# Placing the sums of four groups together in a graph layer: sets, 384-node parts and program order

## The chip, the cores and the metric

One Trainium2 chip, one of its cores. The metric is the device time of one execution in microseconds, the median of several runs. TensorE is called PE, its weight loads PEld, VectorE DVE, ScalarE ACT, GpSimd POOL, SyncE SP.

## What is computed

```python
h = jnp.maximum(_layernorm(x, axis=-1), 0.0)            # x: (12500, 256)
agg = jax.ops.segment_sum(h[src], dst, num_segments=N)  # 200000 edges, dst sorted
z = (1.0 + eps_gin) * h + agg
t = jnp.dot(z, W1) + b1                                 # 256 -> 512
t = jax.nn.relu(_batchnorm(t, g1, bt1))                 # statistics over all nodes
conv_out = jnp.dot(t, W2) + b2                          # 512 -> 256
out = x + jax.nn.relu(_batchnorm(conv_out + h, g2, bt2))
```

All numbers are float32. The edges come sorted by their destination `dst`; `src` is random. A flag computed on the chip selects the function `fast()` where the sorted destinations lie close enough to their expected places, which they do here, and `general()` otherwise.

## The kernel before

The 200000 edges are cut into 1563 tiles of 128 edges and these into 131 groups of 12 tiles (`GT`). Since the destinations are sorted and evenly spread, group `i` touches nodes near `96 * i` (`STEP`); a window of 280 nodes (`WIDE`) with a margin of 76 on the low side holds them. The nodes are cut into 25 chunks of 512 (`CH`) for everything else.

The first part of `fast()` is one loop over the groups, in which all the stages run at once:

- `h_chunk(g)` makes `h` of a chunk: statistics on DVE, 4 activations on ACT (both in `settle`, L328 to L339), a store of `h` to the table `h_tab` in DRAM, 8 transposes on PE (L365), their copies to `hc` on ACT and DVE (L369, L371), and a store of `hc` to `h_cols` by SP's queue (L372).
- `gather(i)` issues 12 indirect DMAs on POOL (L382), one for each tile: 128 rows of 1 KB each into one `gt` buffer, of which there are five (`AHEAD + 1`). The first 24 groups (`LEAD`) read `x` and are normalized by `settle` after they land; the others read `h_tab`.
- `sums(i)` makes a one-hot matrix `oh` of the 12 tiles on DVE (L407) and adds up the rows of equal destination with 12 matmuls (L417) into a PSUM tile `ps`. A float32 matmul gives two records in the trace.
- `join(i)` copies the sums to `zs` on ACT (L424) and makes a second one-hot matrix `at` on DVE (L426) that tells where in the window each destination lies; `put(i)` multiplies the two on PE (L436) into `pz`, which holds the sums by node, in columns.
- `z_chunk(c)` loads a chunk of `h_cols` by SP's queue (L395) and scales it by 1 + eps on ACT (L396); `add(i, pz)` adds `pz` to the one or two chunks that the window meets, on DVE (L449).
- `first_layer(c)` multiplies a complete chunk by W1 (L458), takes statistics on DVE (L462), copies the result on ACT (L463) and stores it to `t_tab` (L464).

The statistics are then aggregated (`norm`, L230 to L241). The second part loads `t_tab` and `h_cols`, normalizes on ACT (L510), multiplies by W2 (L517), adds `h` (L521) and takes statistics (L522). The third part loads `x`, normalizes (L536), transposes back on PE (L542), adds `x` (L548) and stores the output.

The order of the work inside the first part is set by a scheduler that the framework runs when the kernel is built: it may move an instruction on its engine past others of a later call. Waits between engines are semaphores: a tile's reader waits for its writer, and who takes a buffer again waits for its last reader. The lines of the loop are

```python
if i + AHEAD < NG:
    gather(i + AHEAD)
pz = None
if i > 0:
    join(i - 1)
    pz = put(i - 1)
if i < NG:
    if i < LEAD:
        settle(gathered[i], GT // 2, GT, gathered[i], "g")
    sums(i)
```

Of the kernel before, what the change touches and what calls it, by code (L numbers as in the profile page):

```python
# [7 lines left out]
F32 = mybir.dt.float32  # L8
I32 = mybir.dt.int32
# [9 lines left out]
MARGIN = 76  # L19
AHEAD = 4  # L20
# [9 lines left out]
def kernel(  # L30
# [233 lines left out]
    def fast():  # L264

        parts = []
        for n0, w in chunks:
            n = w * R
            parts.append([(c, min(P, n - c * P)) for c in range(-(-n // P))])

        def pieces(g):

            whole = sum(rows == P for _, rows in parts[g])
            yield 0, whole, P
            for c, rows in parts[g][whole:]:
                yield c, c + 1, rows

        def carry(eng, sb, table, g, store):
            n0 = chunks[g][0]
            for c0, c1, rows in pieces(g):  # L280
                if c0 == c1:
                    continue
                side = table[n0 + c0 * P : n0 + (c1 - 1) * P + rows, :].rearrange("(c p) d -> p c d", p=rows)
                if store:
                    eng.dma_start(side, sb[:rows, c0:c1, :])
                else:
                    eng.dma_start(sb[:rows, c0:c1, :], side)

        with ExitStack() as fs:
            keep = fs.enter_context(tc.tile_pool(name="keep", bufs=1))  # L290

            h_cols = dram.tile([NCH, P, DC, CH], F32, name="h_cols")
            t_tab = dram.tile([NCH, P, HC, CH], F32, name="t_tab")
# [4 lines left out]
            with ExitStack() as es:  # L298
# [3 lines left out]
                zcp = es.enter_context(tc.tile_pool(name="zc", bufs=4))  # L302
                tsp = es.enter_context(tc.tile_pool(name="ts", bufs=2))
                ps_h = es.enter_context(tc.tile_pool(name="ps_h", bufs=1, space=PSUM))
                ps_i = es.enter_context(tc.tile_pool(name="ps_i", bufs=1, space=PSUM))
                ps_s = es.enter_context(tc.tile_pool(name="ps_s", bufs=2, space=PSUM))
                ps_z = es.enter_context(tc.tile_pool(name="ps_z", bufs=1, space=PSUM))
                ps_t = es.enter_context(tc.tile_pool(name="ps_t2", bufs=2, space=PSUM))

                col_i = keep.tile([P, WIDE], I32, name="col_i")  # L310
                nc.gpsimd.iota(col_i, pattern=[[1, WIDE]], base=0, channel_multiplier=0)
                col = ps_i.tile([P, WIDE], F32, name="col")
# [7 lines left out]
                nc.vector.tensor_scalar(shift, shift, row, None, op0=OP.add)  # L320
# [24 lines left out]
                def x_chunk(g):  # L345
                    if g >= NCH:
                        return
                    n = chunks[g][1] * R
                    xts[g] = ln.tile([P, R, D], F32, name="xt", bufs=4)
                    if n < CH:  # L350
                        nc.vector.memset(xts[g], 0.0)
                    carry(nc.sync, xts[g], x, g, store=False)

                def h_chunk(g):
                    n = chunks[g][1] * R
                    slots = len(parts[g])
# [3 lines left out]
                    carry(nc.scalar, ht, h_tab, g, store=True)  # L360
                    hc = ln.tile([P, DC, CH], F32, name="hc")
                    for d in range(DC):
                        ph = ps_h.tile([P, CH], F32, name="pc")
                        for c in range(slots):
                            nc.tensor.transpose(  # L365
                                ph[:, c * P : (c + 1) * P], ht[:, c, d * P : (d + 1) * P], ident
                            )
                        if d % 2:
                            nc.scalar.copy(hc[:, d, :n], ph[:, :n])  # L369
                        else:  # L370
                            nc.vector.tensor_copy(hc[:, d, :n], ph[:, :n])  # L371
# [429 lines left out]
```

## Time and profile before

| | |
|---|---|
| median of 3 runs | 2610.4 us (2606.39 to 2611.99) |
| the profiled execution's own time | 2577.98 us |
| its span, first to last instruction | 2576.2 us |
| busy: PE, PEld, DVE, ACT, POOL | 1418.7, 1010.7, 714.3, 460.5, 1482.6 us |
| mean granted PE clock | 0.754 of full speed |
| HBM read, written | 284.26 MB, 64.00 MB |

A row of the costliest groups reads: line, engine, operation, the tiles out<-in, their shape, xcount, then busy us and mean ns of one, then the engine's idle time just before these instructions and what ended most of it. "issue" is time in which the engine waited for nothing that the profile shows; "remote" is a wait whose end the profile can't place with an instruction. A row of the waits reads: who waited <- for whom: us in total, times, the longest. A row of the timeline reads: start, length, engine, line, operation, tiles, xcount, and in brackets the idle time before it and its end. The ends of matmuls are modelled.

### The profile page before, as it was taken

The page shows a single profiled execution, that of the slowest core. Times are in us where ns is not written, and L with a number is a line of the kernel's source. Part 1 is how long each engine was busy: PE and PEld are TensorE (multiplying, and loading weights), DVE is VectorE, ACT ScalarE, POOL GpSimd, SP SyncE. Part 2 cuts the span into 40 slices and gives each one's busy share as a digit, 9 for nine tenths or more (in the row PEclk, how much of TensorE's full clock was granted, in tenths as well). Part 3 has the DMA queues.
Part 4 walks back from the last instruction along what each step waited for, and adds up shares of the span by engine and source line. Part 5 has one row for each costly group of instructions (what it writes and reads, how often), then busy time and mean ns, then how long its engine had stood idle before and what let it go on. Part 6 is the DMA issues. An engine that isn't in the chain of part 4 may idle for free.

```text
span 2576.2 us, 14802 instructions
## 1 busy us (share of the span) xinstructions
PE 1418.7 (55%) x4873; PEld 1010.7 (39%) x4873; DVE 714.3 (28%) x1060; ACT 460.5 (18%) x871; POOL 1482.6 (58%) x1575
## 2 busy tenths in 40 slices
PE   1265566545356455455545554464564555578985
PEld 1243444434244334344333443342443343353444
DVE  4355455222122112221211221221221122133444
ACT  1364566300000000000000000000000000014444
POOL 4666566666666666666666666666666666620000
PEclk6677787777678777777767777676787777788996
DMA  5566675333333333333334333333333333338539
GB/s 164 155 205 201 199 222 171 93 119 113 92 117 118 120 92 119 112 94 116 120 88 122 117 114 95 119 114 92 116 120 119 92 115 101 96 108 319 200 120 319
DMA packets 150067, 349.41 MB, mean 136 GB/s; under 512 B 28920, under 2 KB 84366, under 8 KB 143838
## 3 DMA queue, kind: packets, MB, share of 16 engines
q0 software_dynamic: 75008, 204.90, 27.4%
q1 hardware_dynamic: 44182, 91.21, 10.3%
q10 hardware_dynamic: 30792, 52.26, 5.4%
q8 instruction: 41, 0.67, 0.1%
q14 instruction: 44, 0.36, 0.0%
HBM read 284.26 MB, written 64.00 MB: 135 GB/s over the span
## 4 chain that ended last, share of the span: by engine, by line
another core or an unknown queue 49%; PE 29%; ACT 7%; issue 6%; DVE 4%; DMA 3%; SPq 0%; POOL 0%; ACTq 0%; DVEq 0%; POOLq 0%
PE ps L417 12%; PE py L517 7%; PE pz L436 5%; PE ph L458 4%; ACT gt L339 3%; DMA out_dram<-ot 1%; ACT zs L424 1%; ACT ht L339 1%; DVE oh L407 1%; DVE st L462 1%; DMA zc<-h_cols 1%; DVE zc L449 1%; PE pc L365 1%; ACT ts L463 1%
## 5 line engine op out<-in xcount | busy, mean ns | idle before, releaser
L382 POOL DMA_INDIRECT gt<-h_tab,srcT x1275 | 1207.5, 947 | 608.5 <-issue 370.9
L417 PE MATMUL ps<-gt,oh 128*128 128x256 f32 x3126 | 776.9, 409 | 55.5 <-ACT gt L339 42.8
L417 PEld LDWEIGHTS ps<-gt,oh 128*128 128x128 f32 x3126 | 654.2, 210 | 175.3 <-ACT gt L339 46.6
L436 PE MATMUL pz<-at,zs 128*128 128x280 f32 x524 | 207.2, 531 | 735.3 <-ACT zs L424 578.7
L407 DVE TENSOR_TENSOR oh<-col,dstT 128x1536 f32<-128x1536 f32 x131 | 229.0, 1748 | 1144.1 <-remote 857.0
L436 PEld LDWEIGHTS pz<-at,zs 128*128 128x128 f32 x524 | 119.4, 244 | 796.8 <-ACT zs L424 601.3
L382 POOL DMA_INDIRECT gt<-in_x_dram,srcT x288 | 273.5, 949 | 154.0 <-issue 79.9
L458 PE MATMUL ph<-zc,w1s 128*128 128x512 f32 (+1 forms) x400 | 218.2, 699 | 252.2 <-ACT ts L463 231.9
L424 ACT COPY zs<-ps 128x256 f32<-128x256 f32 x131 | 48.8, 373 | 1633.8 <-remote 1261.3
L458 PEld LDWEIGHTS ph<-zc,w1s 128*128 128x128 f32 x400 | 88.7, 230 | 362.4 <-ACT ts L463 247.0
L449 DVE TENSOR_TENSOR zc<-pz,zc 128x560 f32<-128x560 f32 (+9 forms) x203 | 100.8, 526 | 350.4 <-remote 267.6
L517 PE MATMUL py<-tT,w2s 128*128 128x512 f32 (+1 forms) x400 | 170.9, 590 | 12.0 <-ACT tT L510 12.0
L339 ACT ACTIVATE gt<-gt,nbg,rsg 128x256 f32<-128x256 f32 x288 | 149.5, 590 | 4.0 <-DVE nbg L337 1.9
L517 PEld LDWEIGHTS py<-tT,w2s 128*128 128x128 f32 x400 | 76.8, 193 | 106.0 <-issue 87.2
L462 DVE BATCH_NORM_STATS2 st<-ph 128x6 f32<-128x512 f32 (+1 forms) x100 | 66.6, 679 | 139.5 <-PE ph L458 74.8
L328 DVE BATCH_NORM_STATS2 stg<-gt 128x6 f32<-128x512 f32 x144 | 91.4, 689 | 34.2 <-DMA gt<-in_x_dram,srcT 31.2
L510 ACT ACTIVATE tT<-ti,of,sc 128x512 f32<-128x512 f32 (+1 forms) x100 | 72.0, 791 | 101.1 <-issue 86.7
L463 ACT COPY ts<-ph 128x512 f32<-128x512 f32 (+1 forms) x100 | 57.4, 575 | 181.4 <-DVE st L462 150.4
L426 DVE TENSOR_SCALAR at<-col,shift 128x280 f32<-128x280 f32 x131 | 65.4, 499 | 0.3 <-PE pz L436 0.3
L521 DVE TENSOR_TENSOR yT<-py,yT 128x512 f32<-128x512 f32 (+1 forms) x50 | 33.9, 679 | 110.5 <-PE py L517 108.5
L365 PE MATMUL pc<-ident,ht 128*128 128x128 f32 x196 | 39.2, 334 | 40.6 <-DVE hc L371 16.8
L542 PE MATMUL po<-ident,yr 128*128 128x128 f32 x196 | 40.3, 394 | 33.5 <-ACT yr L536 33.5
(74 smaller groups left out, 382.9 us busy)
## 6 DMA issues: line engine op xcount, KB each, us to landing
t_tab<-ts ACTq DMA_DIRECT2D x24, 1024.0 KB
ti<-t_tab SPq DMA_DIRECT2D x24, 1024.0 KB
gt<-h_tab,srcT POOLq DMA_INDIRECT x1275
xt<-in_x_dram SPq DMA_DIRECT2D x24, 512.0 KB
h_tab<-ht ACTq DMA_DIRECT2D x24, 512.0 KB
h_cols<-hc SPq DMA_DIRECT2D x24, 512.0 KB
zc<-h_cols SPq DMA_DIRECT2D x24, 512.0 KB
yT<-h_cols SPq DMA_DIRECT2D x24, 512.0 KB
```

Source lines behind the costliest of these rows:

```text
L328: nc.vector.bn_stats(st[:, c : c + 2, :].rearrange("p c s -> p (c s)"), v[:, c : c + 2, :].rearrange("p c d -> p d c"),)
L339: nc.scalar.activation(to[:, c, :], v[:, c, :], AF.Relu, bias=nb[:, c : c + 1], scale=rs[:, c : c + 1])
L382: nc.gpsimd.indirect_dma_start(out=ga[:rows, t - t0, :], out_offset=None, in_=x if i < LEAD else h_tab, in_offset=bass.IndirectOffsetOnAxi ...
L407: nc.vector.tensor_tensor(oh[:, :n, :], col[:, :P].unsqueeze(1).to_broadcast([P, n, P]), dstT[:, t0 : t0 + n].unsqueeze(2).to_broadcast([P ...
L417: nc.tensor.matmul(ps, lhsT=oh[:rows, j, :], rhs=ga[:rows, j, :], start=(j == 0), stop=(j == n - 1))
L424: nc.scalar.copy(zs, summed.pop(i))
L436: nc.tensor.matmul(pz[:, d, :WIDE], lhsT=zs[:, d * P : (d + 1) * P], rhs=at, start=True, stop=True)
L449: nc.vector.tensor_add(side, pz[:, :, a - lo : b - lo], side)
L458: nc.tensor.matmul(ph[:, :n], lhsT=w1s[:, d, f * P : (f + 1) * P], rhs=zc[c][:, d, :n], start=(d == 0), stop=(d == DC - 1),)
L462: nc.vector.bn_stats(st1[:, f, c, :], ph[:, :n])
L463: nc.scalar.copy(ts[:, f, :n], ph[:, :n])
L517: nc.tensor.matmul(py[:, :n], lhsT=w2s[:, f, d * P : (d + 1) * P], rhs=tT[:, f, :n], start=(f == 0), stop=(f == HC - 1),)
```

## The change

Four groups in a row form a set (`SET`), and the nodes are cut into 33 parts of 384 (`PART`), shifted by the margin of 76, so that set `s` belongs to part `s`. The six groups whose windows reach into a part (`REACH`) are placed with 12 matmuls into one PSUM tile, each over the blocks of 128 nodes that it can touch; one DVE instruction makes all 12 blocks of the second one-hot matrix (`spots`). `h` is no longer transposed in `h_chunk`: `h_rows` loads the rows of a part from `h_tab` by ACT's queue, `turn` transposes them on PE, `turn_out` copies them, scaled, to `zc` and, unscaled, to `hc` and stores that. `hold` copies the four groups' sums out of PSUM. The first layer works on a part in one PSUM tile of three banks; `take` reads it. `add` is called one set after `place`, and `take` one set after `first_layer`. The one-hot tile `oh` has four buffers instead of two. The scheduler is switched off for the first part (`manual_schedule`): each engine keeps program order. The second and third parts loop over the 33 parts instead of 25 chunks. The diff, cut to its core:

```diff
+SET = 4
...
+        PART = SET * STEP
+        NS = -(-NG // SET)
+        PB = PART // P
+        for j in [0] + [j for j in range(-SET, SET) if j]:
+            lo, hi = max(STEP * j, 0), min(STEP * j + WIDE, PART)
+            if lo < hi:
+                REACH.append((j, lo // P, -(-hi // P)))
...
-                zcp = es.enter_context(tc.tile_pool(name="zc", bufs=4))
-                tsp = es.enter_context(tc.tile_pool(name="ts", bufs=2))
-                ps_h = es.enter_context(tc.tile_pool(name="ps_h", bufs=1, space=PSUM))
+                zcp = es.enter_context(tc.tile_pool(name="zc", bufs=3))
+                tsp = es.enter_context(tc.tile_pool(name="ts", bufs=1))
+                ps_s = es.enter_context(tc.tile_pool(name="ps_s", bufs=SET // 2, space=PSUM))
...
-                ps_s = es.enter_context(tc.tile_pool(name="ps_s", bufs=2, space=PSUM))
                 ps_z = es.enter_context(tc.tile_pool(name="ps_z", bufs=1, space=PSUM))
-                ps_t = es.enter_context(tc.tile_pool(name="ps_t2", bufs=2, space=PSUM))
+                ps_t = es.enter_context(tc.tile_pool(name="ps_t2", bufs=1, space=PSUM))
+                es.enter_context(tc.manual_schedule())
...
-                    xts[g] = ln.tile([P, R, D], F32, name="xt", bufs=4)
+                    xts[g] = ln.tile([P, R, D], F32, name="xt", bufs=3)
...
-                    hc = ln.tile([P, DC, CH], F32, name="hc")
-                    for d in range(DC):
-                        ph = ps_h.tile([P, CH], F32, name="pc")
-                        for c in range(slots):
-                            nc.tensor.transpose(
...
-                    nc.sync.dma_start(h_cols[g, :, :, :n], hc[:, :, :n])
...
-                    oh = sel.tile([P, GT, P], F32, name="oh")
+                    oh = sel.tile([P, GT, P], F32, name="oh", bufs=SET)
...
-                    ps = ps_s.tile([P, D], F32, name="ps")
+                    if i % 2 == 0:
+                        summed[i // 2] = ps_s.tile([P, 2, D], F32, name="ps")
+                    ps = summed[i // 2][:, i % 2, :]
...
+                def h_rows(s):
+                    hrs[s] = ln.tile([P, PB, D], F32, name="hr")
+                    for c in ragged(s):
+                        nc.vector.memset(hrs[s][:, c, :], 0.0)
+                    part(nc.scalar, hrs[s], h_tab, s, store=False)
+                def turn(s):
+                    hr = hrs.pop(s)
+                    hc = ln.tile([P, DC, PART], F32, name="hc")
+                    zc[s] = zcp.tile([P, DC, PART], F32, name="zc")
+                    pz = ps_z.tile([P, DC, CH], F32, name="pz")
+                    for d in range(DC):
+                        for c in range(PB):
+                            nc.tensor.transpose(
+                                pz[:, d, c * P : (c + 1) * P], hr[:, c, d * P : (d + 1) * P], ident
+                            )
+                    turned[s] = hc, pz
+                def turn_out(s):
+                    hc, pz = turned.pop(s)
+                    nc.scalar.activation(zc[s], pz[:, :, :PART], AF.Copy, scale=gin1)
+                    nc.scalar.copy(hc, pz[:, :, :PART])
+                    nc.scalar.dma_start(h_cols[s], hc)
+                    h_rows(s + 2)
+                def hold(s):
+                    for i in range(s * SET, min((s + 1) * SET, NG)):
+                        held[i] = sel.tile([P, D], F32, name="zs", bufs=2 * SET)
+                        nc.scalar.copy(held[i], summed[i // 2][:, i % 2, :])
+                def spots(s):
+                    at = sel.tile([P, PAIRS, P], F32, name="at")
+                    nc.vector.tensor_tensor(
+                        at, col.unsqueeze(1).to_broadcast([P, PAIRS, P]),
+                        spot[:, s, :].unsqueeze(2).to_broadcast([P, PAIRS, P]), op=OP.is_equal,
                     )
...
+                def place(s):
+                    at = ats.pop(s)
+                    placed[s] = ps_z.tile([P, DC, CH], F32, name="pz")
...
                     for d in range(DC):
...
+                        for i, b0, b1, k in some:
+                            nc.tensor.matmul(
+                                placed[s][:, d, b0 * P : b1 * P], lhsT=held[i][:, d * P : (d + 1) * P],
+                                rhs=at[:, k : k + b1 - b0, :].rearrange("p b n -> p (b n)"),
+                                start=(i == some[0][0]), stop=(i == some[-1][0]),
+                            )
+                def add(s):
+                    nc.vector.tensor_add(zc[s], placed.pop(s)[:, :, :PART], zc[s])
+                def first_layer(s):
+                    layers[s] = ps_t.tile([P, HC * PART], F32, name="ph")
                     for f in range(HC):
...
+                        e = f * PART
+                        while e < (f + 1) * PART:
+                            end = min((e // CH + 1) * CH, (f + 1) * PART)
+                            for d in range(DC):
+                                nc.tensor.matmul(
+                                    layers[s][:, e:end], lhsT=w1s[:, d, f * P : (f + 1) * P],
+                                    rhs=zc[s][:, d, e - f * PART : end - f * PART],
+                                    start=(d == 0), stop=(d == DC - 1),
+                                )
+                            e = end
+                def take(s):
+                    ts = tsp.tile([P, HC, PART], F32, name="ts")
+                    a, b = there[s]
+                    ph = layers.pop(s)
+                    for f in range(HC):
+                        nc.vector.bn_stats(st1f[:, f, s, :], ph[:, f * PART + a : f * PART + b])
+                    nc.scalar.copy(ts.rearrange("p f n -> p (f n)"), ph)
+                    nc.scalar.dma_start(t_tab[s], ts)
...
+                for s in range(NS):
+                    for i in range(s * SET, min((s + 1) * SET, NG)):
+                        while made < NCH and made < 3 + NCH * i // (LEAD - AHEAD):
+                            h_chunk(made)
+                            made += 1
+                        if i == 0:
+                            h_rows(0)
+                            h_rows(1)
+                        if i + AHEAD < NG:
+                            gather(i + AHEAD)
                         if i < LEAD:
                             settle(gathered[i], GT // 2, GT, gathered[i], "g")
                         sums(i)
...
+                    spots(s)
+                    if s > 0:
+                        add(s - 1)
+                    if s > 1:
+                        take(s - 2)
+                    turn(s)
+                    hold(s)
+                    turn_out(s)
+                    if s > 0:
+                        first_layer(s - 1)
+                    place(s)
+                add(NS - 1)
+                take(NS - 2)
+                first_layer(NS - 1)
+                take(NS - 1)
...
-                name="ps_o", bufs=3, space=PSUM
+                name="ps_o", bufs=2, space=PSUM
```

## The prediction

> **What bounds the kernel now.** I first read the page's busy shares and its costliest groups. No engine is full, and the row at the top is GpSimd's gather:
>
> ```profile
> PE 1418.7 (55%) x4873; PEld 1010.7 (39%) x4873; DVE 714.3 (28%) x1060; ACT 460.5 (18%) x871; POOL 1482.6 (58%) x1575
> L382 POOL DMA_INDIRECT gt<-h_tab,srcT x1275 | 1207.5, 947 | 608.5 <-issue 370.9
> L417 PE MATMUL ps<-gt,oh 128*128 128x256 f32 x3126 | 776.9, 409 | 55.5 <-ACT gt L339 42.8
> L436 PE MATMUL pz<-at,zs 128*128 128x280 f32 x524 | 207.2, 531 | 735.3 <-ACT zs L424 578.7
> ```
>
> One gather takes 0.947 us and 0.30 us of issue, so 1.252 us start to start; a group of 12 takes 15.03 us, and all 1563 would take 1957 us. They actually run from 32.4 to 2275.4, 2243 us: some 286 us are stops. Second view, busy time by stretch, cut at the events that divide the stages (first gather, first gather from h_tab, last gather, first second-layer matmul, its end):
>
> ```profile
> 32.40:462.70 430.30, 224.46 (x803) 163.97 (x804) 209.21 (x392) 218.08 (x463) 273.49 (x289) 0.72 0.61 193
> 462.70:2275.40 1812.70, 938.47 (x3297) 698.69 (x3297) 371.10 (x473) 125.73 (x243) 1207.43 (x1275) 0.74 0.36 109
> 2275.40:2326.00 50.60, 37.44 (x149) 27.84 (x148) 17.11 (x33) 6.73 (x16) 0.06 (x1) 0.90 0.32 122
> 2326.00:2495.40 169.40, 169.40 (x393) 75.69 (x394) 66.51 (x96) 71.16 (x99) 0.00 (x0) 0.98 0.57 210
> 2495.40:2576.20 80.80, 41.74 (x205) 38.65 (x203) 34.18 (x39) 36.08 (x51) 0.00 (x0) 0.69 0.89 298
> ```
>
> The columns are length, then busy us of PE, weight load, DVE, ACT, POOL, then granted clock, DMA share, GB/s. The 24 groups gathered from x cost 17.9 us each, the 107 from h_tab 16.94 each (67.8 for four). So the second stretch loses 1.9 us a group, 205 us in all, against POOL's pace; that is what there is to win. Third, the waits say who stands there:
>
> ```profile
> ACT zs L424 <- remote: 1261.3, 68, 37.0
> DVE oh L407 <- remote: 857.0, 67, 22.7
> PE pz L436 <- ACT zs L424: 578.7, 57, 36.1
> POOL gt L382 <- remote: 198.2, 41, 6.4
> ```
>
> And the timeline shows one such place:
>
> ```profile
> 1189.83 5.34 PE L417 MATMUL ps<-gt,oh 128*128 128x256 f32 x24
> ...
> 1208.92 0.95 POOL L382 DMA_INDIRECT gt<-h_tab,srcT  x1 [0.30 <-issue]
> 1214.05 0.37 ACT L424 COPY zs<-ps 128x256 f32<-128x256 f32 x1 [25.46 <-remote]
> 1214.05 1.76 DVE L407 TENSOR_TENSOR oh<-col,dstT 128x1536 f32<-128x1536 f32 x1 [22.06 <-remote]
> 1214.29 0.94 POOL L382 DMA_INDIRECT gt<-h_tab,srcT  x1 [4.42 <-remote]
> 1214.48 2.23 PE L436 MATMUL pz<-at,zs 128*128 128x280 f32 x4 [19.30 <-ACT zs L424]
> ```
>
> PE's last sums stand as ended at 1195.2. ACT, DVE and POOL, which all wait for PE there, go on together at 1214.05: 19 us later, and 4.2 us after POOL's last gather ended. This repeats: releases come 2 to 6 us after POOL has stopped, or, in its longest runs of 45 us, once in the middle. So **PE's results are seen late while gathers stream**, by 8 to 22 us in about half of the groups. Each time PE stands with the next placement at its head, which needs ACT's copy of those sums. It runs about four groups behind the gathers, the five gt buffers are full, and POOL stops.
>
> [...] the sums' records start 0.43 us apart after the 19 us wait and 0.2155 later, and the clock averages 0.74. [...] POOL's 1.252 us is a pace that this change leaves alone.
>
> **The change, part by part**, for a set of four groups.
>
> *PE, at full clock.* Sums stay: 96 records at 0.2155 = 20.7. Placement was 16 records of 280 columns at about 0.236, 3.8 us. Now it is 24: eight each of 384, 256 and 128 columns. By columns 0.323 and 0.2155; [...]: 5.8 us. The first layer over 384 nodes was 5.2 (16 records at 0.43 per 512 nodes); in one PSUM tile across bank borders it is also 24 records, 5.8. The six transposes move here from h_chunk, 1.2. Sum 33.5 against 30.9, at clock 0.74 45.3 us, below POOL's 60.1: covered as long as PE isn't kept waiting.
>
> *ACT, DVE, SP and POOL.* From ACT go one hc copy a chunk (0.58) and the zc scaling of a loaded tile (1.15); it gains two copies of 768 columns (0.87 each, between its 0.585 and 1.145 rows) and one ts copy of 1536 instead of four (about 1.4). DVE makes one at of 1536 columns (1.76) for four of 280 (4 x 0.50), one add of 768 (about 0.95) for some six of 0.526, and no hc copy. Both were busy 371 and 126 of 1813 us in the second stretch: nothing there. SP loses the h_cols store and zc load, ACT's queue gains the h_tab load and h_cols store, at 0.33 to 0.46 us an issue, about 1 us a set. The bytes cancel (one 12.8 MB read for another). POOL is moved past nothing.
>
> *Waits.* oh has four buffers, so the one-hot waits for sums four groups back. add(s-1) and take(s-2) read PE results a set, some 60 us, old, longer than any lag seen. But hold(s) and turn_out(s) still read results that PE has just issued, and place(s) needs both. That is **one late wait a set instead of up to one a group**. Behind place in PE's order stand the next four sums, and POOL waits for their buffers. The lag W is bounded by 0 and 22 us; first_layer(s-1), 7.8 us at clock 0.74, now lies in front of place and covers that much. The copies before place are 4 x 0.373 + 2 x 0.87 = 3.2. So PE's set is 45.3 + 3.2 + W = 48.5 + W; with 8 to 22 less the cover, W is 0 to 14 and PE needs 49 to 63. POOL needs 60.1, plus 4.1 for a stop. Full rounds of stops give 64.2, none 60.1. I take half: 62.2. The 26.75 sets then take 1664 instead of 1813: **-149**.
>
> *The first stretch.* ACT and DVE keep program order through chunk, group and set. A chain of one group: 12 activations 7.1, the chunk's stretch with four of 0.59 beside six DVE statistics of 0.69, about 4.3, four hand-overs 1.6, a quarter chunk more, 0.8; a set's copies and its wait for sums and transposes, some 15, add 3.8. That is 17.6 against 17.9; bounds 16.5 to 20, so -34 to +50. I take +8, since each hold may also meet a lag.
>
> *The end.* After the last gather, 50.6 now: first_layer(31) and place(32) stand before the last add, take and first layer, and four aggregations read 198 instead of 150 numbers: about +6. Second layer: 528 records at 0.323 = 170.5 against 169.4. Output is at 89% DMA share with the same bytes: +1, between 0 and +8 since two po buffers replace three. Together +8.
>
> The profiled execution took 2578.0 us around its span of 2576.2, 32 below the median of 2610.4; I make the sum on the profile's terms and apply it to the median: 2610 - 149 + 8 + 8 = **2477, given as 2475**. Its own range is 2440 (lags vanish in most sets, 61) to 2540 (a stop in every set, 64.2, and a slower first stretch).
>
> **The rivals.** *POOL at its own pace*: 60.1 a set, -205 + 16: 2420; 2385 if the first stretch falls to 16.5. For it: before, releases came in mid-stream in every run of 45 us, and a buffer may wait some 45 us for its release here. Against: PE still has one fresh result to wait for, and no stretch of gathers over 45 us without a stop is seen.
>
> *PE becomes the bound, slower than before*: the sums' results lag 22 us in each set, and the first layer covers nothing because its own PSUM or add is late. Then PE needs 48.5 + 22 = 70.5 against 67.8 now: 26.75 x 2.7 = +72, with the +8 +8: 2698. It decides from W = 19.3 on. For it: hold, turn_out and place follow each other in one set, nothing else may be put into the gap under program order, and a clock at half makes the work itself 67. Against: the lag ended each time POOL stopped, and then everything older is released at once.
>
> *The set order doesn't matter*: lags are short but the five gt buffers still fill, one stop per two groups: 60.1 + 8.2 = 68.3, time 2610 + 13 + 16 = 2640.
>
> **Numbers.** Chances: the likeliest 0.48, POOL's pace 0.18, PE bound 0.24, no gain from the set 0.10. A measurement of this kernel can tell about 0.2%, 5 us, from no change. Faster 0.66; of the last case 0.03 falls within; slower 0.31. The range leaves a tenth on each side: 2385 to 2680.
>
> **What would show it.** Right: stops of POOL (idle before L382 beyond the 0.30 issue) fall from 286 us to about 130; stretches of 48 gathers with at most one stop; ACT's remote wait before zs drops to one per set; PE's wait stands in front of place. Wrong: the four-group period stays at 68 or more, with PE's idle time before place above 19 us a set; or the stretch from x takes over 480 us; or the end after the last gather takes over 320.

## The result, and the profile after

The changed kernel takes 2692.0 us (2688.8 to 2695.7) against 2608.4 (2606.4 to 2612.0): **3.2% slower**, ratio 1.0319, interval 1.0299 to 1.0340. The forecast was 2475.

One fact is needed to read the later numbers. The same two kernels were measured again, and whole series of runs came out in one of two conditions: in one the kernel before takes 2594 to 2614 us, as on record; in the other 2271 to 2272 us. I call them **held** and **free**; the traces below show why. Chips 1, 6 and 12 were seen free, 11 and 12 held, so the condition isn't the chip. The pair on record is held. Every number below stands beside the kernel before of its own series.

The profiled execution of after spans 2693.5 us. Its page, first the busy line, then the costliest groups (count, busy us and mean ns, then the engine's idle us just before them and what ended it):

```profile
PE 1565.6 (58%) x5653; PEld 1138.9 (42%) x5653; DVE 641.3 (24%) x853; ACT 476.4 (18%) x868; POOL 1480.9 (55%) x1577
L412 POOL DMA_INDIRECT gt<-h_tab,srcT x1275 | 1204.9, 945 | 726.3 <-issue 373.7
L436 PE MATMUL ps<-gt,oh 128*128 128x256 f32 x3126 | 753.1, 402 | 214.1 <-issue 157.2
L512 PE MATMUL ph<-zc,w1s 128*128 128x256 f32 (+2 forms) x792 | 304.3, 474 | 494.3 <-issue 488.2
L495 PE MATMUL pz<-at,zs 128*128 128x384 f32 (+2 forms) x780 | 268.4, 501 | 329.9 <-ACT hc L466 140.3
```

GpSimd's busy time is what it was, its idle time is 118 us longer. PE's wait in front of the placement fell from 735 to 330 us. The first layer stood like this before:

```profile
L458 PE MATMUL ph<-zc,w1s 128*128 128x512 f32 (+1 forms) x400 | 218.2, 699 | 252.2 <-ACT ts L463 231.9
```

Its 252 us have become 494, and nearly all of it is now put down to issue: no wait for a semaphore shows in front of these matmuls. Busy time by stretch, same cuts and columns as before:

```profile
32.00:447.70 415.70, 216.24 (x728) 163.26 (x728) 187.12 (x339) 212.22 (x439) 273.86 (x288) 0.77 0.53 169
447.70:2378.60 1930.90, 1084.71 (x4001) 802.98 (x4001) 318.62 (x286) 128.17 (x216) 1204.87 (x1275) 0.72 0.36 108
2378.60:2432.30 53.70, 40.10 (x169) 30.66 (x169) 11.83 (x24) 10.16 (x15) 0.01 (x1) 0.90 0.42 153
2432.30:2604.30 172.00, 171.95 (x528) 100.95 (x528) 73.48 (x132) 81.56 (x131) 0.31 (x1) 0.99 0.59 210
2604.30:2693.50 89.20, 45.44 (x198) 35.27 (x198) 34.55 (x42) 41.54 (x67) 0.31 (x1) 0.64 0.81 267
```

The difference of the spans, 117 us, is -15 in the stretch from x, **+118 in the stretch from h_tab** (72.2 us for four groups, was 67.8) and +14 after the last gather. By the medians it is 84 us: the profiled execution of before, 2578 us, is 30 us shorter than its median, so some 33 us of the 117 are scatter between executions. The waits:

```profile
ACT zs L473 <- remote: 1044.8, 29, 45.0
DVE oh L424 <- remote: 861.7, 44, 37.5
PE ph L512 <- issue: 488.2, 314, 3.1
POOL gt L412 <- PE ps L436: 219.4, 16, 17.7
```

ACT's late wait is one a set now, as the change promises, but up to 45 us long. The timeline of PE shows what happens between; start and length in us:

```profile
1193.51 22.20 PE L436 MATMUL ps<-gt,oh 128*128 128x256 f32 x96
1215.55 0.82 PE L458 MATMUL pz<-ident,hr 128*128 128x128 f32 x6
1216.20 1.79 PE L512 MATMUL ph<-zc,w1s 128*128 128x384 f32 x7
1218.79 0.27 PE L512 MATMUL ph<-zc,w1s 128*128 128x128 f32 x1 [0.80 <-issue]
...
1237.69 0.37 PE L512 MATMUL ph<-zc,w1s 128*128 128x128 f32 x1 [2.43 <-issue]
1240.49 0.37 PE L512 MATMUL ph<-zc,w1s 128*128 128x128 f32 x1 [2.43 <-issue]
1243.29 0.37 PE L512 MATMUL ph<-zc,w1s 128*128 128x128 f32 x1 [2.43 <-issue]
...
1253.19 7.63 PE L495 MATMUL pz<-at,zs 128*128 128x384 f32 x24 [2.11 <-ACT hc L466]
```

96 records of sums pass in 22 us; then single records, their starts 0.70 us or a multiple of it apart (2.80 five times in a row), though no wait for a semaphore shows. GpSimd's last gather of this run ends at 1245.15, and 8 us later the placement's 24 records pass in 7.6 us.

### The profile page after: what moved, and what is told of

It is laid out like the page before. It is cut to its first block, busy times and chain, and to the rows that moved or that the text cites. A ratio compares the mean times of both kernels' runs of the same rounds, so it can differ in the third digit from the quotient of the medians.

```text
span 2693.5 us, 16122 instructions
## 1 busy us (share of the span) xinstructions
PE 1565.6 (58%) x5653; PEld 1138.9 (42%) x5653; DVE 641.3 (24%) x853; ACT 476.4 (18%) x868; POOL 1480.9 (55%) x1577
## 4 chain that ended last, share of the span: by engine, by line
another core or an unknown queue 41%; PE 32%; issue 12%; ACT 6%; DVE 4%; DMA 2%; POOL 2%; ACTq 0%; DVEq 0%; POOLq 0%
PE ps L436 14%; PE pz L495 9%; PE py L588 6%; ACT gt L381 2%; POOL gt L412 2%; PE ph L512 2%; DVE stg L370 2%; DMA out_dram<-ot 1%; ACT zs L473 1%; ACT zc L465 1%; ACT hc L466 1%; DVE oh L424 0%; PE po L614 0%; DMA xr<-in_x_dram 0%
## 5 line engine op out<-in xcount | busy, mean ns | idle before, releaser
L512 PE MATMUL ph<-zc,w1s 128*128 128x256 f32 (+2 forms) x792 | 304.3, 474 | 494.3 <-issue 488.2
L495 PE MATMUL pz<-at,zs 128*128 128x384 f32 (+2 forms) x780 | 268.4, 501 | 329.9 <-ACT hc L466 140.3
L512 PEld LDWEIGHTS ph<-zc,w1s 128*128 128x128 f32 x792 | 168.3, 231 | 594.9 <-issue 570.3
L495 PEld LDWEIGHTS pz<-at,zs 128*128 128x128 f32 x780 | 177.1, 252 | 452.0 <-issue 193.7
L588 PE MATMUL py<-tT,w2s 128*128 128x384 f32 x528 | 172.0, 489 | 7.2 <-ACT tT L581 7.2
L526 ACT COPY ts<-ph 128x1536 f32<-128x1536 f32 x33 | 47.4, 1438 | 446.8 <-DVE st1f L525 364.0
L581 ACT ACTIVATE tT<-ti,of,sc 128x384 f32<-128x384 f32 x132 | 82.4, 695 | 83.5 <-issue 82.7
L525 DVE BATCH_NORM_STATS2 st1f<-ph 128x6 f32<-128x384 f32 (+2 forms) x132 | 63.6, 544 | 8.8 <-PE ph L512 8.8
L381 ACT ACTIVATE ht<-xt,nbc,rsc 128x256 f32<-128x256 f32 x98 | 50.9, 589 | 53.3 <-DVE nbc L379 26.2
L592 DVE TENSOR_TENSOR yT<-py,yT 128x384 f32<-128x384 f32 x66 | 36.8, 558 | 97.1 <-PE py L588 91.9
```

What stands on the lines that cost most here:

```text
L381: nc.scalar.activation(to[:, c, :], v[:, c, :], AF.Relu, bias=nb[:, c : c + 1], scale=rs[:, c : c + 1])
L495: nc.tensor.matmul(placed[s][:, d, b0 * P : b1 * P], lhsT=held[i][:, d * P : (d + 1) * P], rhs=at[:, k : k + b1 - b0, :].rearrange("p b n ...
L512: nc.tensor.matmul(layers[s][:, e:end], lhsT=w1s[:, d, f * P : (f + 1) * P], rhs=zc[s][:, d, e - f * PART : end - f * PART], start=(d == 0 ...
L525: nc.vector.bn_stats(st1f[:, f, s, :], ph[:, f * PART + a : f * PART + b])
L526: nc.scalar.copy(ts.rearrange("p f n -> p (f n)"), ph)
L581: nc.scalar.activation(tT[:, f, :], ti[:, f, :], AF.Relu, bias=of1[:, f : f + 1], scale=sc1[:, f : f + 1],)
```

## The experiments

Theory 1, the forecast's and its second rival's: one late result in front of the placement, a fixed wait a set. Theory 2: while gathers stream without a break, PE gets almost nothing through, whatever is in its queue; what counts is how much it must do between two breaks.

**The pair again, and four edits, all free.** First the changed and the old kernel themselves.

> The changed kernel itself, to have it beside the kernel before where the first four experiments ran, with the kernel before at 2271 us instead of 2608. Two conditions are possible. If TensorE's instructions are held back while gathers stream, as in the traces of before and after: 2692 us against 2608, ratio 1.03. If they are not, as in the first four experiments (not one stop of GpSimd over 0.4 us in the h_tab stretch): 24 and then 106.9 groups at 15.0 us each bound it, the gathers end at 1986 us and the end of about 302 to 315 us follows: 2280 to 2300 us, ratio 1.005 to 1.012.

> The kernel before itself, for a profile of it in the condition of these runs. If TensorE is held back: 2608 us and 54 stops of GpSimd in the h_tab stretch. If not: no stops there, gathers at 15.0 us a group, their last at about 1980 us, an end of 290 to 300 us, 2271 us.

Measured: 2288.8 us and 2272.7 us; the ratio of after to before is 1.0074 (1.0057 to 1.0090). GpSimd's row of before, then of after, and PE's timeline of after:

```profile
L382 POOL DMA_INDIRECT gt<-h_tab,srcT x1275 | 1207.0, 947 | 388.5 <-issue 384.6 <-DMA gt<-h_tab,srcT 1.8 <-PE ph L458 0.9
```

```profile
L412 POOL DMA_INDIRECT gt<-h_tab,srcT x1275 | 1206.7, 946 | 388.6 <-issue 387.6 <-DMA gt<-h_tab,srcT 0.6 <-DVE zc L502 0.3
```

```profile
1056.32 8.34 PE L436 MATMUL ps<-gt,oh 128*128 128x256 f32 x24 [7.68 <-DMA gt<-h_tab,srcT]
1064.49 0.82 PE L458 MATMUL pz<-ident,hr 128*128 128x128 f32 x6
1065.15 5.37 PE L512 MATMUL ph<-zc,w1s 128*128 128x384 f32 x24
1070.35 5.36 PE L495 MATMUL pz<-at,zs 128*128 128x384 f32 x24
```

Neither has a stop; both are bound by gathers of 1.25 us, and PE waits for them. In the same program, the first layer's 24 records start within 4.9 us (median of the 27 sets in the h_tab stretch; held 33.3), and the copy of the set's last sums starts 0.30 us after them (held 34.8). So the order of after holds no wait of its own: **the stops, and what the change does about them, exist only in the held condition.** The 16 us that remain lie after the last gather.

```
-                    if s > 0: first_layer(s - 1)     # e1_place_first
                     place(s)
+                    if s > 0: first_layer(s - 1)
```

> The changed kernel, with the first layer of the set before put behind the placement instead of ahead of it. Theory 1 (the forecast's own picture): the 7.8 us of the first layer cover part of the wait for the copied sums in front of the placement; without them the wait grows by that, 7.8 us in each of the 26.6 sets of the h_tab stretch, about +200 us: 2890 us. Theory 2 (after about 15 to 20 us of unbroken gathers TensorE gets only one instruction through per 0.7 us or slower, whatever the instruction is, and its results are seen late): the first layer covers nothing, so the order is worth little: 2690 us, within 30 us. In the trace the placement then takes the stretched issue that the first layer has now.

```
-                            for d in range(DC):      # e2_half_first, later e15_half_first
+                            for d in range(1):
```

> The changed kernel without the second half of the first layer's contraction: it makes 6 matmuls a set instead of 12, so its first layer is incomplete. Theory 1 (a late result in front of the placement costs a fixed wait each set): only TensorE's own time goes, 2.9 us at full clock, 3.9 us at the granted 0.74, less what it covered: between 0 and -3.9 us a set, 2590 to 2690 us. Theory 2 (TensorE's instructions are held to a slow pace while the gathers stream): the 12 records that go were issued at 1.4 us and more apart, so about 15 us a set go until the gathers bound: 72.4 to 61 us a set, about 2400 us, and the stops of GpSimd fall from 394 us to under 150.

```
                     for t in reversed(range(t0, t0 + n)):      # e4_half_gathers
+                        if i >= LEAD and (t - t0) % 2: continue
...
-  rhs=ga[:rows, j, :]
+  rhs=ga[:rows, j - j % 2 if i >= LEAD else j, :]
```

> The changed kernel with every second gather of the h_tab groups left out; the sums read the tile beside it instead, so these sums are of the wrong rows, but TensorE, VectorE and ScalarE do just what they did. GpSimd needs 30 us a set. Theory 1 (order alone: one late result in front of the placement): TensorE's set stays at about 70 us, the time at 2640 to 2690 us. Theory 2 (streaming gathers slow TensorE): the gathers pause most of the time, TensorE's set costs its own 45 us at the granted clock and a short wait, 46 to 52 us: h_tab stretch 1230 to 1380 us instead of 1931, the time 1990 to 2150 us, and the first layer's idle time put down to issue (488 us) falls under 100 us.

```
+                        if i == s * SET + 1:           # e5_later, in the loop over groups
+                            hold(2 * s - 1); spots(s - 1); add(s - 2); take(s - 3)
+                            turn(s); turn_out(s)
...
+                    hold(2 * s)                        # by pairs of groups
+                    first_layer(s - 2)
+                    place(s - 1)
```

> The changed kernel with everything that reads a result of TensorE put half a set to a set later still: the sums are copied half a set late, the transposes are made in mid-set, the placement takes sums that are all half a set old or older, the one-hot tables are made two groups ahead. No instruction of TensorE reads a result that is fresh. Theory 1 (a wait for a fresh result in front of the placement is the whole loss): that wait is gone, TensorE needs 45 us a set and GpSimd bounds: 60 to 63 us a set, h_tab stretch about 1640 us, the time 2370 to 2420 us. Theory 2 (TensorE's instruction pace falls while the gathers stream, and this sets how much it does between two pauses): it still has 150 records a set to issue, and the time moves little: 2600 to 2700 us.

```
-                es.enter_context(tc.manual_schedule())   # e6_sched
```

> The changed kernel without the line that keeps each engine in program order: the scheduler may put each engine's instructions where it likes. Where TensorE is held back: theory 1 (an order with a wait in it) gives a time away from the 2692 us of the changed kernel, 2600 us or less if the scheduler moves the placement behind the next sums; theory 2 (the count of instructions between pauses) gives the same within 1.5%. Where TensorE isn't held back, the gathers bound and the order is worth nothing but in the end: within 10 us of the changed kernel.

Measured 2287.8 (ratio to before 1.0070), 2282.5 (1.0051), 1552.2 (0.6836), 2303.9 (1.0142) and 2284.2 us (1.0050). Free, neither order nor count nor the scheduler is worth 1%: GpSimd hides all. They don't tell the theories apart, since the thing to explain wasn't there. The half gathers do show PE's own need, in this stretch:

```profile
393.00:1231.00 838.00, 830.34 (x3906) 697.47 (x3906) 309.75 (x273) 120.78 (x198) 603.01 (x638) 0.99 0.48 150
```

838 us are 31.3 us for each of 26.75 sets, at clock 0.99. That is less than the 33.5 of the forecast and half of GpSimd's 60.

**A lag made on purpose, held.** These four were written for the free condition and met the held one.

```
                     for t in reversed(range(t0, t0 + n)):      # e9_before_half, on before
+                        if i >= LEAD and (t - t0) % 2: continue   # sums read the tile beside
```

> The kernel before with every second gather of the h_tab groups left out, its sums reading the tile beside instead (the sums are of the wrong rows; TensorE, VectorE and ScalarE do what they did). The counterpart of the same cut in the changed kernel, which took 1552 us with 31.5 us a set of four groups in the h_tab stretch, TensorE 99% busy there. By the forecast's sums the kernel before needs 30.9 us of TensorE for four groups against 33.5: if TensorE alone bounds both, 28 to 29 us for four groups, 1552 - 26.6 x 2.6 - 17 for the end = about 1465 us. If the kernel before has waits between its groups that the gathers hid, up to 2 us a group: 1500 to 1680 us. Where TensorE is held back while gathers stream, both numbers rise; then only the two beside each other in the same condition count.

```
+                        nc.scalar.copy(slow[:, :D], summed.pop(i))   # e10 on before: 6 times, each group
+                        for _ in range(6): nc.scalar.copy(slow, slow) # e11, e12: 26 times, each set
+                        nc.scalar.copy(zs, slow[:, :D])
```

> The kernel before with the copied sums of each h_tab group made late on purpose: ScalarE copies them into a scratch tile, copies that onto itself 6 times (about 1.5 us each), and takes the sums from there: about 9 us of lag for each group, some 36 for four. It asks what a late result costs each order where TensorE's own issue isn't held back. TensorE waits in front of each placement: 6.3 us of sums, 9.5 of lag and copy, 1.2 of placement, about 1.6 of first layer beside it: 16.2 to 17.8 us a group against 15.0 of the gathers: +1.2 to 2.8 us in 106.9 groups: 2400 to 2570 us.

> The changed kernel with the copied sums of each h_tab set made late on purpose in the same way: 26 copies of 1536 elements on ScalarE, about 38 us of lag for each set, the median lag of the trace of the changed kernel being 34.8. TensorE's set at the 0.82 granted here: 25.2 of sums, 38 + 3.2 of lag and copies, beside which the transposes and the first layer (7.4) lie, 7.1 of placement: 72 to 75 us against 60.1 of the gathers: +12 to 15 us in 26.6 sets: 2600 to 2690 us. If so, the forecast's picture of one wait in front of the placement, with the first layer inside it, is right where TensorE issues freely, and the 2692 us on record can be had from a late result alone. If the buffers of the gathers let the wait hide: 2290 us.

> The half-set-late version of the changed kernel (nothing on TensorE reads a fresh result) with the same 38 us of lag in every h_tab set. If the order is what makes a late result cost time, it hides here: 2304 us as without the lag, within 15 us. If a late result costs in any order (sums need the bank that the late copy frees): TensorE reaches the sums of the third group 39 us after the set's end, then 12.6 of two groups and 13 of transposes, first layer and placement: 65 us a set, +130 us: 2430 us.

Measured 1780.9 (0.6857), 2683.1 (1.0343), 3603.0 (1.3889) and 2731.0 us (1.0514), before at 2594.3. The first can't be set beside the free 1552. In the second, 9 us of lag a group cost only 89 us in all. The third is far from its 2600 to 2690: 102.6 us a set in the h_tab stretch. Its waits:

```profile
ACT slow L475 <- remote: 1199.6, 24, 51.8
PE pz L502 <- ACT hc L468: 1118.7, 27, 45.5
```

ACT learns of the sums 50 us late, and only then do its 26 copies (1.471 us each, 38.2) begin: the two add, 30 us a set more than after. So after has no room at all for a late result when held. The fourth, in which PE reads nothing fresh, hides the same 38 us: its h_tab stretch (475.6 to 2351.3) takes 70.1 us a set, less than after without any lag. But it doesn't come down to 60, and PE's idle time is put down to issue, in the first layer as much as in after:

```profile
L529 PE MATMUL ph<-zc,w1s 128*128 128x256 f32 (+2 forms) x792 | 292.7, 468 | 533.3 <-issue 495.4 <-ACT ts L543 36.1
L512 PE MATMUL pz<-at,zs 128*128 128x384 f32 (+2 forms) x780 | 272.2, 480 | 228.5 <-issue 222.2 <-ACT slow L485 4.0
```

**Theory 1 alone falls**: with no fresh result to wait for, 10 us a set are still lost. How much of the 10 is the lag's isn't known, since this order was not measured held without it.

**Fewer instructions, more buffers, a forced pause, held.** Before at 2613.6. After itself was not measured in this series; its 2692 us below is that of the result, at 1.0319.

```
-  layers[s] = ps_t.tile([P, HC * PART], ...)         # e13_wide; pieces cut at bank borders
+  layers[s] = ps_t.tile([P, HC, CH], ...)            # one piece of 384 for each f
-  col = ps_i.tile([P, P], ...)
+  col = keep.tile([P, P], ...)
```

> The changed kernel with each quarter of the first layer in a bank of its own, so in one piece of 384 columns: 8 matmuls a set (16 records) instead of 12 (24), the same columns in all; the table of column numbers moves from PSUM to SBUF to make room. Where TensorE is held back (kernel before at about 2600 us): theory 2 (what counts is the number of instructions issued after the gathers have streamed for some 20 us, 1.4 us for a record and more) gives 8 records x 1.4 = 11 us less a set until other stops bound, 72.4 to 61 to 66 us a set: 2400 to 2540 us; a theory that counts TensorE's time (fewer columns don't change) gives 2680 us. Where it isn't held back the gathers bound: 2289 us within 8.

> The changed kernel without the second half of the first layer's contraction (6 of 12 matmuls a set; its first layer is incomplete), once more, for a chip that holds TensorE back. There: theory 2 gives 12 records at 1.4 us and more, 15 us a set less until other stops bound: 2300 to 2480 us; theory 1 (the wait in front of the placement is all, and TensorE's own 3.9 us go) 2590 to 2690 us. Elsewhere 2282 us as before.

Measured 2629.9 (1.0066, 1.0041 to 1.0091) and 2637.0 us (1.0091, 1.0062 to 1.0119): 55 to 62 us ahead of after, and both above the 2540 and 2480 that theory 2 allowed at most: a price of 1.4 us for each record left out is refuted. Where the loss went is the useful part. Groups of the wide one (e13):

```profile
L435 PE MATMUL ps<-gt,oh 128*128 128x256 f32 x3126 | 1015.3, 460 | 854.9 <-issue 703.2 <-ACT gt L380 76.3 <-DMA gt<-h_tab,srcT 47.3
L508 PE MATMUL ph<-zc,w1s 128*128 128x384 f32 x528 | 183.6, 498 | 15.2 <-issue 10.5 <-ACT ts L520 4.5
L411 POOL DMA_INDIRECT gt<-h_tab,srcT x1275 | 1329.3, 1043 | 519.0 <-issue 378.5
```

The first layer's 488 us for issue have become 10, and the sums' 157 have become 703; the columns of the first layer are the same. The slow time isn't bound to an instruction: it moved to what now stood in the queue. Something else is new here: the gathers themselves take 1043 ns in the mean, because 137 of them took 1.17 to 2.52 us instead of 0.95. That is 122 us of the h_tab stretch, so the time of the wide version isn't PE's alone. Why they are slow is open. With half a first layer the loss moved to the wait instead:

```profile
ACT zs L473 <- remote: 1043.7, 28, 45.0
PE pz L495 <- ACT hc L466: 681.7, 22, 46.7
```

```
+                    if i >= LEAD and i % 2:           # e16_pause, also e3_pause; e17: range(3)
+                        for _ in range(6): nc.gpsimd.memset(rest, 0.0)     # 128 x 1024
```

> The changed kernel, with six memsets of 128 x 1024 elements on GpSimd after the gathers of every second h_tab group: about 6 to 7 us without a gather, taken from the row of the 128 x 256 memset (0.31 us), 53 times. If TensorE is held back while gathers stream (theory 2): the pauses replace the stops, TensorE's issue runs at full pace in and after each of them, and the set takes 60 + 13 = 73 us, as before them: 2690 us, within 40 us, and waits of GpSimd for the sums nearly go. If a late result in front of the placement is the loss (theory 1): the pauses come on top of part of the stops: 2720 to 2850 us. Where TensorE isn't held back the pauses only add: 53 x 6.5 = 345 us on the time of the changed kernel.

> The changed kernel with a pause of 5.9 us in GpSimd's gathers after every second group of the h_tab stretch (six memsets), once more, for a chip that holds TensorE back. Elsewhere it took 2598 us: the pauses' 309 us on top of 2289, with not one other stop. On such a chip: if 30 us of gathers between two pauses leave TensorE enough time at full pace, it catches up in each pause and takes the same 2598 us, less than the 2692 us of the changed kernel; then forced pauses cost less than the stops that they replace. If TensorE falls behind all the same, pauses and stops add: 2750 to 2950 us.

Free: 2597.7 us, the pauses' 309 on top. Held: **2664.0 us** (1.0205, 1.0146 to 1.0265), less than after though it gives away 319 us. GpSimd's row, and PE's timeline around a run of gathers from 1210.2 to 1240.0:

```profile
L413 POOL DMA_INDIRECT gt<-h_tab,srcT x1275 | 1208.0, 947 | 390.9 <-issue 380.7 <-ACT gt L381 9.5 <-DMA gt<-h_tab,srcT 0.6
```

```profile
1205.21 0.59 PE L440 MATMUL ps<-gt,oh 128*128 128x256 f32 x1 [1.51 <-issue]
1207.32 8.59 PE L440 MATMUL ps<-gt,oh 128*128 128x256 f32 x24 [1.51 <-issue]
1227.01 7.14 PE L440 MATMUL ps<-gt,oh 128*128 128x256 f32 x24 [11.11 <-DMA gt<-h_tab,srcT]
...
1262.81 4.05 PE L440 MATMUL ps<-gt,oh 128*128 128x256 f32 x17 [1.61 <-DMA gt<-h_tab,srcT]
1267.20 0.47 PE L440 MATMUL ps<-gt,oh 128*128 128x256 f32 x1 [0.34 <-issue]
1270.01 0.59 PE L440 MATMUL ps<-gt,oh 128*128 128x256 f32 x2 [1.73 <-issue]
```

Gathers stop at 1204.1 (six memsets follow) and PE is fast 3.2 us later; the next run starts at 1246.2 and PE slows 21 us into it. With a break every 30 us PE caught up wholly: it waits for gathers (590 us in all), and GpSimd has almost no stop left but the forced ones (two more, 10 us together). So theory 2 holds in kind.

Is it the length of streaming that counts, or how much PE issues in it? The traces can be counted for this. I call PE slowed in a run of gathers where a matmul record stood over 0.3 us for issue; a gap over 1.6 us between two gathers ends a run.

| trace, runs of gathers | matmul records that PE starts in a run | slowed | records before that | time before that |
|---|---|---|---|---|
| pauses, held (e16), 26 runs of 29.7 us | 85 to 92 | 22 | 78 to 89 | 19 to 26 us |
| pauses, held (e16), 25 runs of 29.7 us | 38 to 58 | 0 | | |
| pauses, free (e3), 53 runs of some 30 us | 37 to 92 | 0 | | |
| after, held, 26 runs of 45 or 60 us | 90 to 100 | 26 | 74 to 85 | 16 to 20 us |
| after, free, 1 run of 1595 us | 4014 | 0 | | |

In each of the 25 held runs with few records, PE still started 16 records more than 20 us into the run. So the length alone doesn't slow it; a count of what PE has issued since the break fits. Held, one of the long runs of after lets about 95 records through, whether it lasts 45 us or 60. (In 8 of its 19 runs of 15 us PE is slowed too, some records in, so a short break may leave something over from the run before.) As an estimate from these figures, after needs more than one and a half runs a set, since a set has 150 records. That would explain why it loses: 34% of the gathers of before lay in runs of over 40 us (counted from start to start), 81% of after. It is read from the traces; no experiment changed the count and the length apart. The wide version fits only in part: in 20 of its 25 runs PE slows after 97 to 124 records, and its runs, 64 us in the median, are longer than those of after.

```
-  xin bufs=6, ysb bufs=3, ps_o bufs=2               # e14_tail, last part alone
+  xin bufs=8, ysb bufs=4, ps_o bufs=4
```

> The changed kernel with more buffers in its last stage alone: 8 for x rows instead of 6, 4 for the results instead of 3, 4 pairs of banks for the last transposes instead of 2. Its last stage took 88 us against 78 of the kernel before, with 0.82 of the DMA engines' time against 0.88. If the buffers of smaller parts (384 rows for 512) hold it back: 6 to 10 us less than the changed kernel, 2280 us where the gathers bound (2672 where TensorE is held back). If the count of transfers and of instructions does: within 2 us of the changed kernel.

Measured 2696.9 us (1.0333, 1.0276 to 1.0390); the h_tab stretch scattered by 8 us against the recorded profile, which swamps the whole. The last part by itself, cut as above, decides:

```profile
2617.30:2696.60 79.30, 43.77 (x198) 35.17 (x198) 34.58 (x42) 41.55 (x67) 0.31 (x1) 0.66 0.90 302
```

79.3 us against 89.2, DMA share 0.90 against 0.81: the buffers were the loss there, and 10 us come back.

**Short or spread breaks.** Meant for held, met free, so their question wasn't answered.

```
+                        if i >= LEAD: nc.gpsimd.memset(rest[:, :48], 0.0)   # e18_spread, after each gather
```

> The changed kernel with the pause after every second h_tab group halved: three memsets, 2.9 us, 53 times, 155 us in all. On a chip that holds TensorE back the pauses of 5.9 us (313 us in all) left not one other stop and TensorE waited 590 us for gathers, so it had time to spare. If 2.9 us are enough for TensorE to come up again: 5.7 us of pause a set, 65.9 us a set: 2664 - 155 = 2510 us, ahead of both kernels there. If the break must outlast the about 5 us after which TensorE went fast again in the stops of the changed kernel: it falls behind, pauses and stops together as long as the stops now, 2660 to 2800 us. Where TensorE isn't held back: 2289 + 155 = 2444 us.

> The changed kernel with the same GpSimd time spread out: one memset of 128 x 48 elements, about 0.12 us, after each gather of the h_tab stretch, 1275 of them, about 150 us in all, and no pause. On a chip that holds TensorE back: if the rate of the gathers is what holds it (a tenth fewer a us), TensorE keeps up better and the time is 2450 to 2560 us; if it is unbroken streaming for more than some 20 us, the stops come as in the changed kernel, shorter by what the slower pace gives: 2650 to 2750 us. Where TensorE isn't held back: about 2440 us.

Measured 2435.1 (1.0717) and 2317.0 us (1.0194). The short pauses cost their own 146 us. The spread memsets cost 28, not 150: most of each fits into the 0.30 us of issue between gathers (start to start 1.273 for 1.251).

No version beats both kernels: free, before is ahead of all that keep its work; held, the wide one comes nearest at 1.0066. Its first layer was not measured together with the buffers of the last part.

## Why the prediction was wrong

**GpSimd's pace, 15.03 us a group:** right, in both conditions. **Results are seen late:** right in kind, 34.8 us where 8 to 22 were taken; I had read the lag as a property of the result, when PE's issue was slowed as well. **One late wait a set:** right, 29 waits of ACT.

**The failing step is "first_layer(s-1), 7.8 us at clock 0.74, now lies in front of place and covers that much", and with it "W is 0 to 14".** The first layer covered nothing: it stands in the held time itself, and its 24 records took 33.3 us to start instead of 4.9. Cut to the h_tab stretch, PE's idle time inside the first layer and in front of the placement is (487.4 + 328.0) / 26.75 = 30.5 us a set. Of these the sum had foreseen 3.2 for the copies, so 27 us stand where it put W at 0 to 14. That is above the 19.3 from which the second rival said the change loses. PE's own work was cheaper than the 45.3 of the sum: it was busy for 40.5 us a set, and 40.5 + 30.5 + 1.2 of other idle time make the 72.2. Three fifths of the 30.5 lie in the first layer's issue, where neither the forecast nor the rival looked.

That the rival's 2698 us lies within 7 of the result is in part luck. It took +72 for the h_tab stretch, where the spans show +118, and +8 for the stretch from x, where they show -15; and the profiled execution that its working starts from was 32 us below the median to which it was applied.

Behind that stands an assumption the text never priced: that PE's speed doesn't depend on how much it has issued since GpSimd's last break. The rhythm of before, a break about every two groups, kept PE going: in its 27 runs of some 30 us PE started 55 to 72 records. The change lets runs of 45 and 60 us form. I cited "no stretch of gathers over 45 us without a stop is seen" against the fastest rival only. "Stops of POOL fall from 286 us to about 130": by the same sum (2378.6 - 32.0 - 1957) they rose to 390.

**The first stretch, +8 within -34 to +50:** measured -15, inside the bounds. Free, 361.2 and 361.9 us, it makes no difference. **The end, +8:** +14. The term that was mis-sized is the output, "+1, between 0 and +8": +8.4, and the buffers are its cause. **PE's need, 33.5 us:** 31.3 at clock 0.99. Part of the difference lies in the 128-column records of the placement and the first layer: in the trace of after, where no idle time comes between, the next record starts 0.112 us later in the median; the sum's 5.8 us leave 0.19 for each.

*Open:* what brings the held condition, and by what path gathers slow PE; no run here shows either. Every execution on record was itself recorded, each has a granted clock, so whether an unrecorded one is ever held can't be told. Slow fetching of instructions doesn't show: the transfers on queue q8, which the trace calls instruction, 16 KB each and 47 in each trace of after, took 0.98 us in the median held and 1.07 free. Whether a break under 6 us is enough when held wasn't seen.

## What to carry to other kernels

Matmuls that don't issue cover no wait: held, the first layer's 24 records, counted as 7.8 us of cover, took 33.3 us to start. So look for idle time put down to issue on instructions that wait for nothing, and count no cover there. Before a change is made to remove the stops of a streaming engine, ask who works in those stops; here, held, they were PE's time, and with a forced pause of 6 us every 30 us PE waited 590 us for gathers. Count what an engine must issue between two stops, and not only how long it is busy: after had 150 records a set to start, and held about 95 passed in a run. Measure the pair in more than one series of runs, since what a change repairs may exist in one of them alone: after to before was 1.032 held and 1.007 free.

## What the hardware showed that I hadn't expected

- The same program took 2692 us held and 2289 us free, 15% less, with GpSimd's gather at 0.945 and 0.946 us. Only in the wide version, held, did the gathers themselves grow, to 1.043 us in the mean.
- Held, PE goes fast from 3 to 8 us after the gathers pause until it has started some 80 matmul records (74 to 89 in after and with the pauses), then mostly a record every 0.7 to 2.8 us. Its last results reach the others late: at 1251.0 in a pause of the gathers from 1245.2, but also at 1299.6 in the middle of a run. In the median of the 27 sets of the h_tab stretch, ScalarE's copy of a set's last sums starts 34.8 us after they stand as ended.
- Held, with runs of gathers of 15 us in the median (before with every second gather left out), the placement stood 20 us for issue and 196 us for late copies in all, against 156 and 579 in the recorded run.
